# Bias seeded into PSUM by ScalarE, and the last batches reordered, in a two-layer graph attention kernel

## The chip, the cores and the metric

The kernel runs on one core of a Trainium2 chip. The metric is the device time in microseconds of one execution; lower is better. The engines are named as in the profile: PE (TensorE, matrix products), DVE (VectorE), ACT (ScalarE), POOL (GpSimd), SP (SyncE, which here issues nearly all DMAs). Each engine works through its own instructions in program order [...].

## The reference, cut to what matters

The input `x` holds 128 batches of 128 tokens with 512 features, all in 32-bit floats. With `B = 128`, `L = B - 1` and `ln` a normalization over the features without weights, the reference computes for every batch:

```
y  = ln(x + relu(max_over_features(adj @ x) + b))       # layer 0
q, k, v = split(y @ w_qkv)                              # 8 heads of 64
p  = softmax(where(adj == 0, -inf, q k^T / 8))
o  = concat_heads(p v) @ w_proj + b_proj
z  = y + o + ln(o) * gamma + beta                       # layer 1
out = ln(z)
```

Only the last part of this concerns the change: the projection `o`, its bias `b_proj`, the inner normalization of `o`, the residual sum, and the outer normalization of `z`.

## The kernel before, in words

Batches go in groups of four (`G = 4`, `NG = 32` groups). The products with the weights are done for a whole group by a scheme that replaces eight block products by seven (class `Unit`, lines 165 to 194): `product(i)` adds one of seven products into one of the PSUM banks `b1` to `b4`, `snap(k)` copies the running sum in `b1` to SBUF on ACT, and `result(half, col)` adds a bank and a snap on DVE. The left operands of a unit for `o` are sums of blocks that POOL makes (`o_sums`, line 495).

For one batch `scores` (line 385) makes the scores on PE, `softmax_max` adds the mask and takes the maximum on DVE, `softmax_exp` runs one exponential per head on ACT, `softmax_div` divides on DVE, `prob_transpose` transposes 32 by 32 blocks on DVE, `prob_write` and `prob_read` finish the transposition through DRAM with DMAs on SP's queue, `attend` (line 471) multiplies with `v` on PE and `attend_copy` copies the result to SBUF on ACT. `prob_move` is the three middle steps together; its read waits on SP for its write to land, and everything later on SP waits with it.

The end of a batch is a row of tail steps. `bn` and `finish_stats` (lines 245 to 269) take mean and variance on DVE and turn them into a scale and a shift, mostly on POOL, where `ALU.pow` gives the inverse root. `tail_inner_one` (line 599) normalizes `o` on ACT, `tail_residual_one` (line 603) has three steps on POOL: times gamma, plus `o`, plus the saved row that a DMA has brought back. `tail_outer_one` (line 622) normalizes `z` on ACT and stores it. For the very last batches `fused_open` and `fused_close` (lines 608 to 620) do the inner normalization and the residual sum on DVE instead.

A loop over pairs of batches (line 730) does this until four pairs from the end, with the bias added by POOL. The last part, from line 888, is written out by hand: a list of calls whose order is the order of the instructions on each engine, since `pin` keeps program order. There the bias is added on PE: `biased` (line 891) follows products 2, 5 and 4 of the units `o_u` with two products each of a row of ones and the bias, and `last_project` (line 518), which projects one of the last four batches alone, ends with `add_bias` (line 515). Before those, `last_load` (line 509) and ten `tail_reload_one` calls bring `w_proj` and ten saved rows into one buffer, through SP's queue.

PSUM has eight tiles by tag: `b1` to `b4` of the units, `pss0`, `pss1`, `po`, `pa` of scores and attention. A new tile of a tag waits until the old one has been read. The last four batches are projected into `b2`, `pss0`, `pss1` and `b1`.

The order of the tails before the change: the statistics `last_1` (line 962) take two rows of `z` and four of `o` together, ahead of `attend(L - 5)`; then normalizing and residual steps of L-11 to L-8 in the next stretch, L-5 and L-4 after `attend(L - 2)`, L-7 and the fused L-3, L-2, L-6, L-1 and L to the end.

Of the kernel before, what the change touches and what calls it, by code (L numbers as in the profile page):

```python
# [16 lines left out]
def kernel(  # L17
# [55 lines left out]
    def pe(*args, **kwargs):  # L73
        pin(nc.tensor.matmul(*args, **kwargs))  # L74

    def tt(eng, dst, a, b, op):
        pin(eng.tensor_tensor(dst, a, b, op))  # L77
# [71 lines left out]
    make_identity(nc, ident)  # L149
    mhalf = const.tile([P, 1], F32, name="mhalf")  # L150
    pin(nc.gpsimd.memset(mhalf, -0.5))
    ones = const.tile([1, P], F32, name="ones")
    pin(nc.gpsimd.memset(ones, 1.0))

# [8 lines left out]
    class Unit:  # L165
# [6 lines left out]
            self.banks, self.snaps = {}, {}  # L172

        def product(self, i):
            bank, first = {1: (1, True), 6: (1, False), 7: (1, False), 2: (2, True),
                           5: (3, True), 3: (3, False), 4: (4, True)}[i]
            if first:
                self.banks[bank] = psum.tile(
                    [P, 2, HT], F32, tag=f"b{bank}", name=f"b{bank}_{self.name}"
                )  # L180
            self.mm(self.banks[bank], i - 1, self.lefts[i], first)

        def snap(self, k):
            t = sb.tile([P, 2, HT], F32, tag=f"u{k}", name=f"u{k}_{self.name}")
# [200 lines left out]
    def scores(b, banks=("pss0", "pss1")):  # L385
        g, h, jj = place(b)
        pss[b] = [
            psum.tile([P, NP, P], F32, tag=tag, name=f"pss{par}_{b}")
            for par, tag in enumerate(banks)
        ]  # L390
        for pr in range(NP):
            for par in range(2):
                t = qk[g, pr // 2, h][ds(par * HD, HD), :, pr % 2, ts(jj, P)]
                pe(pss[b][par][:, pr], lhsT=t[:, 0], rhs=t[:, 1], start=True, stop=True)
# [71 lines left out]
    def prob_move(b):  # L466
        prob_transpose(b)
        prob_write(b)
        prob_read(b)
# [15 lines left out]
    def attend_copy(b):  # L485
        g, h, jj = place(b)
        if jj == 0:
            tag = "x" if (g, h) == (NG - 2, 0) else "oT"
            oT[g, h] = sb.tile([P, KC, HT], F32, tag=tag, name=f"oT_{g}_{h}", bufs=2)
        pin(nc.scalar.copy(oT[g, h][:, :, ts(jj, P)], pos.pop(b)))  # L490
# [15 lines left out]

    def last_load():
        t = sb.tile(WQK, F32, tag="wqk", name="wlast")  # L510
        w = t[:, :2].rearrange("p a b e -> p (a b) e")
        pin(nc.sync.dma_start(out=w, in_=w_proj.rearrange("(c p) e -> p c e", p=P)))
        return w, t[:, 2:].rearrange("p a b e -> p (a b) e")

    def add_bias(dst, cols):
        pe(dst, lhsT=ones, rhs=bp_bc[0:1, cols], start=False, stop=True, skip_group_check=True)

    def last_project(b, w, tag):
        g, h, jj = place(b)
        ps = psum.tile([P, D], F32, tag=tag, name=f"pp_{b}")  # L520
        for c in range(KC):
            pe(
                ps,
                lhsT=oT[g, h][:, c, ts(jj, P)],
                rhs=w[:, c],
                start=c == 0,
                stop=True,
                skip_group_check=True,
            )
        add_bias(ps, slice(0, D))  # L530
        os_[b] = ps


    zs, xr = {}, {}
# [92 lines left out]
    def stats(name, *items, eng=None, fused=0):  # L627

        mv = small.tile([P, NC, 2], F32, tag="mv", name=f"mv_{name}")
        for k, (kind, b) in enumerate(items):  # L630
            bn({"o": o_of, "z": zs.get, "y": xs.get}[kind](b), mv, k)
        finish_stats(mv, items, eng, fused)
        return mv


    for f, tag in enumerate(("pa", "po", "b3", "b4")):
# [250 lines left out]

    L = B - 1
    po_pa = ("po", "pa")

    def biased(unit, i):

        unit.product(i)
        bank, cols = {2: (2, slice(0, HE)), 5: (3, slice(HE, D)), 4: (4, slice(0, HE))}[i]
        for k in range(2):
            add_bias(unit.banks[bank][:, k], cols)


    before, o_u, v_u = second, o_unit(NG - 3), v_unit(NG - 1)
# [2 lines left out]
    attend_copy(L - 7)  # L902
    attend(L - 6, "pa")
    attend_copy(L - 6)
    scores(L - 5)
    scores(L - 4, po_pa)
    before.result(1, 1)
# [3 lines left out]
    softmax_max(L - 4)  # L911
    o_u.product(1)
    o_u.snap(1)
    biased(o_u, 2)
    softmax_exp(L - 5)
    o_u.result(0, 0)
    before.product(3)
    before.result(0, 1)
    tail_residual(B // 2 - 7)
    o_u.product(6)  # L920
    scores(L - 3)
    softmax_exp(L - 4, range(4))
    o_u.snap(2)
    softmax_exp(L - 4, range(4, H))
    softmax_div(L - 5)
    prob_move(L - 5)
    biased(o_u, 5)
    softmax_max(L - 3)
    scores(L - 2, po_pa)
    biased(o_u, 4)  # L930
    o_u.product(7)
    softmax_exp(L - 3, range(4))
    o_u.snap(3)
    softmax_exp(L - 3, range(4, H))
# [9 lines left out]
    for t in range(L - 9, L + 1):  # L944
        tail_reload_one(t, room[:, t - L + 9])
    v_u.product(2)
    v_u.product(1)
    v_u.snap(1)
    o_u.product(3)
    softmax_exp(L - 2, range(4))  # L950
    o_u.result(0, 1)
    v_u.result(0, 0)
    v_u.product(6)
    v_u.snap(2)
    softmax_exp(L - 2, range(4, H))
    v_u.product(5)
    v_u.product(4)
    v_u.product(7)
    softmax_div(L - 3)
    prob_transpose(L - 3)  # L960
    prob_write(L - 3)
    stats(
        "last_1",
        ("z", L - 13), ("z", L - 12), ("o", L - 11), ("o", L - 10), ("o", L - 9), ("o", L - 8),
    )


    attend(L - 5)
    v_u.snap(3)
    attend_copy(L - 5)  # L970
    attend(L - 4, "pa")
    attend_copy(L - 4)
    prob_read(L - 3)
    scores(L - 1)
    v_u.result(1, 1)
    run_sums(o_sums(NG - 2))
    for t in range(L - 11, L - 7):
        tail_inner_one(t)
    softmax_max(L - 1)
    scores(L, po_pa)  # L980
    v_u.result(1, 0)
    o_u = o_unit(NG - 2)
    o_u.product(1)
    o_u.snap(1)
    biased(o_u, 2)
    softmax_div(L - 2)
    prob_move(L - 2)
    softmax_exp(L - 1)
    softmax_max(L)
    o_u.result(0, 0)  # L990
    v_u.product(3)
    v_u.result(0, 1)
    for t in range(L - 11, L - 7):
        tail_residual_one(t)
    o_u.product(6)
    softmax_exp(L, range(4))
    o_u.snap(2)
    softmax_exp(L, range(4, H))
    biased(o_u, 5)
    biased(o_u, 4)  # L1000
    o_u.product(7)
    softmax_div(L - 1)
    prob_move(L - 1)
    softmax_div(L)
    prob_move(L)
    attend(L - 3)
    o_u.snap(3)
    attend_copy(L - 3)
    attend(L - 2, "pa")
    attend_copy(L - 2)  # L1010
    tail_outer(B // 2 - 7)
    tail_store(B // 2 - 7)
    mv = small.tile([P, NC, 2], F32, tag="mv", name="mv_last_2")
    keys = [("z", L - 11), ("z", L - 10), ("o", L - 5), ("o", L - 4)]
    bn(zs[L - 11], mv, 0)
    bn(zs[L - 10], mv, 1)
    o_u.result(1, 1)
    o_u.result(1, 0)
    bn(o_of(L - 5), mv, 2)
    bn(o_of(L - 4), mv, 3)  # L1020
    pool = nc.gpsimd
    finish_stats(mv, keys, pool)
    for t in (L - 5, L - 4):
        tail_inner_one(t)
    for t in (L - 11, L - 10):
        tail_outer_one(t)
    tail_residual_one(L - 5, [0])
    o_u.product(3)
    o_u.result(0, 1)
    last_project(L - 3, wlast, "b2")  # L1030
    last_project(L - 2, wlast, "pss0")
    attend(L - 1)
    attend(L, "pa")
    mv2 = stats("last_3", ("o", L - 6), ("o", L - 7), eng=pool, fused=1)
    tail_inner_one(L - 7)
    tail_residual_one(L - 5, [1])
    mv = stats("last_4", ("o", L - 3), ("z", L - 9), eng=pool, fused=1)
    tail_outer_one(L - 9)
    fused_open(L - 3, mv[:, 0, 0:1])
    tail_residual_one(L - 5, [2])  # L1040
    fused_close(L - 3)
    attend_copy(L - 1)
    attend_copy(L)
    last_project(L - 1, wlast, "pss1")
    last_project(L, wlast, "b1")
    tail_residual_one(L - 4, [0])
    mv = stats("last_5", ("o", L - 2), ("z", L - 3), ("z", L - 8), eng=pool, fused=1)
    fused_open(L - 2, mv[:, 0, 0:1])
    for t in (L - 3, L - 8):
        tail_outer_one(t)  # L1050
    tail_residual_one(L - 4, [1, 2])
    fused_open(L - 6, mv2[:, 0, 0:1])
    fused_close(L - 2)
    fused_close(L - 6)
    tail_residual_one(L - 7, [0])
    mv = stats("last_6", ("o", L - 1), ("z", L - 2), ("z", L - 5), eng=pool, fused=1)
    fused_open(L - 1, mv[:, 0, 0:1])
    for t in (L - 2, L - 5):
        tail_outer_one(t)
    tail_residual_one(L - 7, [1, 2])  # L1060
    fused_close(L - 1)
    mv = small.tile([P, NC, 2], F32, tag="mv", name="mv_last_7")
    keys = [("o", L), ("z", L - 1), ("z", L - 4), ("z", L - 6)]
    for k in (2, 3, 1):
        bn(zs[keys[k][1]], mv, k)
    bn(o_of(L), mv, 0)
    finish_stats(mv, keys, pool, fused=1)
    fused_open(L, mv[:, 0, 0:1])
    for t in (L - 1, L - 4, L - 6):
        tail_outer_one(t)  # L1070
    fused_close(L)
    stats("last_8", ("z", L), ("z", L - 7), eng=pool)
    for t in (L, L - 7):
        tail_outer_one(t)


# [39 lines left out]
```

## Time and profile before

| | |
|---|---|
| median of 3 runs | 1969.37 us (1969.04 to 1970.28) |
| profiled execution, its own time | 1968.16 us |
| span of the profiled execution | 1966.4 us |
| granted TensorE clock, mean | 0.997 |
| busy share of the span: PE, DVE, ACT, POOL | 99%, 80%, 54%, 66% |
| last product on PE starts | 1950.69 us |
| last instruction on ACT starts | 1962.09 us |

The times of the profile are microseconds from the start of the span. A row of a timeline has the start, the duration, the engine, the line of the code (often that of a helper: line 74 is every product, line 77 every tensor-tensor operation), the operation, the tile written and the tiles read, the shape, how many instructions are merged into the row, and in brackets how long the engine was idle before it and what released it. Products of 32-bit operands appear as two instructions each. In rows of groups, "busy us, mean ns" is the total and the duration of one.

### The profile page before, as it was taken

The numbers are of one execution on the slowest core, as the hardware profiler recorded it, in microseconds if no ns is written. First come the engines' busy times: TensorE is split into PE (matmuls) and PEld (weight loads), VectorE is DVE, ScalarE is ACT, GpSimd is POOL, SyncE is SP. The second block draws the span as 40 slices with busy tenths as digits, with TensorE's granted clock in tenths as the row PEclk, the third lists the DMA queues.
The fourth block names the chain that finished last, engine by engine and source line by source line (L and its number), as shares of the span: only waits on it lengthen the run. The fifth ranks groups of instructions, "written<-read, shape, count | busy, mean of one in ns | idle before, by whom it ended". The sixth has DMA issues, their size and how long they took to land.

```text
span 1966.4 us, 33091 instructions
## 1 busy us (share of the span) xinstructions
PE 1945.3 (99%) x11575; PEld 1642.5 (84%) x11575; DVE 1564.2 (80%) x2516; ACT 1054.6 (54%) x3066; POOL 1294.2 (66%) x815
## 2 busy tenths in 40 slices
PE   9999999999999999999999999999999999999996
PEld 6888888888888888888888888888888888888883
DVE  6767878878778778788788787787787887877777
ACT  3444654655555546546556555555465465555463
POOL 6336766767666767667676667676676776676737
PEclk9999999999999999999999999999999999999998
DMA  7647567576576676676675765765766766757544
GB/s 223 169 121 191 145 177 193 155 189 175 164 197 162 168 200 160 169 194 157 185 189 157 191 167 166 203 161 164 198 157 180 189 161 187 174 162 189 150 167 144
DMA packets 445654, 341.75 MB, mean 174 GB/s; under 512 B 276912, under 2 KB 378416, under 8 KB 445488
## 3 DMA queue, kind: packets, MB, share of 16 engines
q1 hardware_dynamic: 445056, 338.85, 64.4%
q8 instruction: 92, 1.51, 0.3%
q10 hardware_dynamic: 432, 0.79, 0.1%
q14 instruction: 74, 0.61, 0.1%
HBM read 172.82 MB, written 166.72 MB: 173 GB/s over the span
## 4 chain that ended last, share of the span: by engine, by line
PE 95%; DVE 2%; POOL 2%; DMA 0%; ACT 0%; issue 0%; SPq 0%; ACTq 0%; POOLq 0%; DVEq 0%
PE b_qk L74 40%; PE b_v L74 19%; PE b_o L74 19%; PE pss L74 6%; PE po L74 6%; PE pa L74 5%; POOL zl L77 1%; DVE st_mv_last L247 1%; POOL s_o L77 0%; POOL rs_mv_last L77 0%; DMA x<-in_x_dram 0%; PE idle L74 0%; DVE mv_last L248 0%; ACT s L419 0%; DVE z L620 0%
## 5 line engine op out<-in xcount | busy, mean ns | idle before, releaser
L74 PE MATMUL b_qk<-s_x,wqk 128*128 128x256 f32 x2048 | 473.4, 379 | 0.6 <-DVE s_x L77 0.3
L74 PEld LDWEIGHTS b_qk<-s_x,wqk 128*128 128x128 f32 x2048 | 388.8, 190 | 55.1 <-issue 0.9
L419 ACT ACTIVATE s<-s,nmax 128x128 f32<-128x128 f32 x1024 | 396.1, 391 | 6.7 <-DVE nmax L412 6.7
L74 PE MATMUL b_qk<-x1T,wqk 128*128 128x256 f32 x1536 | 358.8, 383 | 0.1
L74 PEld LDWEIGHTS b_qk<-x1T,wqk 128*128 128x128 f32 x1536 | 286.6, 190 | 45.2 <-issue 1.0
L77 POOL TENSOR_TENSOR z<-z,ga_bc 128x1024 f32<-128x1024 f32 x58 | 164.5, 2836 | 168.5 <-ACT z L273 168.5
L259 POOL TENSOR_SCALAR rs_mv<-mv 128x6 f32<-128x6 f32 (+2 forms) x61 | 14.7, 241 | 380.9 <-DVE mv L248 380.9
L77 DVE TENSOR_TENSOR s<-s,rec 128x1024 f32<-128x1024 f32 x128 | 252.9, 1976 | 4.4
L185 ACT COPY u_qk<-b_qk 128x512 f32<-128x512 f32 x192 | 112.4, 585 | 245.4 <-PE b_qk L74 244.1
L74 PE MATMUL b_v<-wv,s_x 128*128 128x256 f32 x1024 | 237.0, 379 | 0.0
L74 PE MATMUL b_o<-wp,s_o 128*128 128x256 f32 x992 | 230.1, 380 | 0.5 <-DVE v L191 0.5
L74 PEld LDWEIGHTS b_v<-wv,s_x 128*128 128x128 f32 x1024 | 194.4, 190 | 26.8 <-issue 0.3
L191 DVE TENSOR_TENSOR qk<-b_qk,u_qk 128x512 f32<-128x512 f32 x256 | 168.2, 675 | 56.7 <-PE b_qk L74 44.4
L400 DVE SCALAR_TENSOR_TENSOR s<-pss,mask 128x512 f32<-128x512 f32 x256 | 164.3, 684 | 59.4 <-PE pss L74 59.1
L74 PEld LDWEIGHTS b_o<-wp,s_o 128*128 128x128 f32 x992 | 188.1, 190 | 27.2 <-DVE v L191 0.9
L77 POOL TENSOR_TENSOR x<-x,be_bc 128x1024 f32<-128x1024 f32 x64 | 181.3, 2834 | 33.5 <-DVE rec L430 27.4
L419 ACT ACTIVATION_READ_ACCUMULATOR s<-s,nmax 128x1 f32 x1024 | 193.9, 189 | 0.0
L191 DVE TENSOR_TENSOR v<-b_v,u_v 128x512 f32<-128x512 f32 x128 | 87.1, 681 | 133.9 <-PE po L74 129.1
L185 ACT COPY u_o<-b_o 128x512 f32<-128x512 f32 x93 | 54.4, 585 | 247.0 <-PE b_o L74 247.0
L185 ACT COPY u_v<-b_v 128x512 f32<-128x512 f32 x96 | 56.2, 585 | 238.4 <-PE b_v L74 238.4
L74 PE MATMUL b_v<-wv,x1T 128*128 128x256 f32 x768 | 176.2, 379 | 0.0
L74 PEld LDWEIGHTS b_v<-wv,x1T 128*128 128x128 f32 x768 | 145.9, 190 | 32.2 <-issue 13.9
(115 smaller groups left out, 3403.9 us busy)
## 6 DMA issues: line engine op xcount, KB each, us to landing
hop<-pu SPq DMA_DIRECT2D x128, 512.0 KB, 3.4
pT<-hop SPq DMA_DIRECT2D x512, 128.0 KB, 3.7
spill<-x SPq DMA_DIRECT2D x64, 512.0 KB, 4.8
x<-in_x_dram SPq DMA_DIRECT2D x62, 512.0 KB, 4.4
xhop<-xt SPq DMA_DIRECT2D x248, 128.0 KB, 2.3
x1T<-xhop SPq DMA_DIRECT2D x248, 128.0 KB, 3.9
xr<-spill SPq DMA_DIRECT2D x59, 512.0 KB, 3.5
out_dram<-xr SPq DMA_DIRECT2D x58, 512.0 KB, 4.1
```

Of the source, the lines that this page charges most:

```text
L74: pin(nc.tensor.matmul(*args, **kwargs))
L77: pin(eng.tensor_tensor(dst, a, b, op))
L185: pin(nc.scalar.copy(t, self.banks[1]))
L191: nc.vector.tensor_tensor(self.out[half, col], self.banks[bank], self.snaps[k], ALU.add)
L247: pin(nc.vector.bn_stats(st, src))
L259: pin(nc.gpsimd.tensor_scalar(rs[:, :n], mv[:, :n, 1], EPS, None, ALU.add))
L400: nc.vector.scalar_tensor_tensor(s[:, par], pss[b][par], SCALE, mask.unsqueeze(1).to_broadcast([P, NP, P]), ALU.mult, ALU.add,)
L419: nc.scalar.activation(prob[b][:, i], prob[b][:, i], AF.Exp, bias=nmax[b][:, i : i + 1], accum_out=psums[b][:, i : i + 1],)
```

## The change

The row of ones goes. ScalarE writes the bias into a PSUM bank before the products, [...] no product into such a bank carries the start flag. `seed` does so for banks 2, 4 and 3 of the two last `o_u` units, `last_seed` for the banks of the last four batches, which are now `b2`, `b4`, `b3` and `b1`.

Two statistics of `z` (L-8 and L-11) are taken on ACT: `scalar_stats` runs an Identity with a sum, a mean, and a Square of the deviation with a sum, and `finish_scalar_stats` ends them on POOL. The outer normalization of the last batch goes from ACT to DVE (`tail_outer_vector`). The hand-written list is reordered. The inner normalization and the residual steps of L-9 and part of those of L-8 move ahead of `attend(L - 5)`; the statistics are cut into more and smaller groups that POOL finishes; `softmax_div(L - 2)` and its transposition and write come before `attend(L - 5)`; the scores of L-2 and of L come earlier; `attend(L - 1)` and `attend(L)` come ahead of `last_project(L - 2)`, and their copies come behind the statistics on ACT. L-8 and L-11, then L-10, are normalized later than before.

```diff
-    def add_bias(dst, cols):
-        pe(dst, lhsT=ones, rhs=bp_bc[0:1, cols], start=False, stop=True, skip_group_check=True)
-
-    def last_project(b, w, tag):
+    def seed(unit, bank):
+        cols = slice(HE, D) if bank == 3 else slice(0, HE)
+        bias = bp_bc[:, cols].unsqueeze(1).to_broadcast([P, 2, HE])
+        pin(nc.scalar.copy(unit.new_bank(bank), bias))
+
+    def last_seed(b, tag):
+        os_[b] = psum.tile([P, D], F32, tag=tag, name=f"pp_{b}")
+        pin(nc.scalar.copy(os_[b], bp_bc))
...
-                start=c == 0,
+                start=False,
...
-        add_bias(ps, slice(0, D))
-        os_[b] = ps
...
+    def tail_outer_vector(b, mean):
+        z, (rs, _) = zs.pop(b), stat_of.pop(("z", b))
+        pin(nc.vector.tensor_scalar(z, z, mean, rs, ALU.subtract, ALU.mult))
+        pin(nc.sync.dma_start(out=out[b], in_=z))
+
+    def scalar_stats(*batches):
...
+        for k, b in enumerate(batches):
+            pin(act(trash, zs[b], AF.Identity, accum_out=sums[:, k : k + 1]))
+        pin(act(mean[:, :n], sums[:, :n], AF.Identity, scale=-1.0 / D))
+        for k, b in enumerate(batches):
+            pin(
+                act(
+                    trash, zs[b], AF.Square, bias=mean[:, k : k + 1], accum_out=dev[:, k : k + 1]
+                )
+            )
+        return batches, mean, dev
+
+    def finish_scalar_stats(stat):
+        batches, sh, rs = stat
+        n = len(batches)
+        pin(nc.gpsimd.tensor_scalar(rs[:, :n], rs[:, :n], 1.0 / D, EPS, ALU.mult, ALU.add))
+        tt(nc.gpsimd, rs[:, :n], rs[:, :n], mhalf.to_broadcast([P, n]), ALU.pow)
+        tt(nc.gpsimd, sh[:, :n], sh[:, :n], rs[:, :n], ALU.mult)
...
+    seed(o_u, 2)
     scores(L - 5)
...
-    biased(o_u, 2)
+    o_u.product(2)
     softmax_exp(L - 5)
+    seed(o_u, 4)
...
+    softmax_exp(L - 4, range(4))
     o_u.product(6)
     scores(L - 3)
-    softmax_exp(L - 4, range(4))
+    scores(L - 2, po_pa)
     o_u.snap(2)
+    seed(o_u, 3)
     softmax_exp(L - 4, range(4, H))
     softmax_div(L - 5)
     prob_move(L - 5)
-    biased(o_u, 5)
+    o_u.product(4)
+    o_u.product(5)
+    o_u.product(7)
     softmax_max(L - 3)
-    scores(L - 2, po_pa)
-    biased(o_u, 4)
-    o_u.product(7)
...
+    stats("last_1", ("o", L - 9), ("o", L - 8), eng=pool)
...
+    for t in (L - 9, L - 8):
+        tail_inner_one(t)
+    tail_residual_one(L - 9)
     v_u.product(5)
-    v_u.product(4)
     v_u.product(7)
+    stats("last_2", ("o", L - 11), ("o", L - 10), eng=pool)
+    tail_residual_one(L - 8, [0])
     softmax_div(L - 3)
...
+    softmax_div(L - 2)
+    prob_transpose(L - 2)
+    prob_write(L - 2)
...
+    o_u.product(5)
+    o_u.product(7)
     softmax_exp(L, range(4, H))
-    biased(o_u, 5)
-    biased(o_u, 4)
-    o_u.product(7)
+    o_u.snap(3)
+    o_u.product(4)
...
+    o_u.product(3)
+    o_u.result(0, 1)
+    last_project(L - 3, wlast)
+    for t, tag in ((L - 2, "b4"), (L - 1, "b3"), (L, "b1")):
+        last_seed(t, tag)
+    attend(L - 1)
+    attend(L, "pa")
+    last_project(L - 2, wlast)
+    stat = scalar_stats(L - 8, L - 11)
+    finish_scalar_stats(stat)
     for t in (L - 5, L - 4):
         tail_inner_one(t)
...
     attend_copy(L - 1)
     attend_copy(L)
-    last_project(L - 1, wlast, "pss1")
-    last_project(L, wlast, "b1")
+    last_project(L - 1, wlast)
+    last_project(L, wlast)
...
     mv = small.tile([P, NC, 2], F32, tag="mv", name="mv_last_8")
     keys = [("o", L), ("z", L - 1), ("z", L - 4)]
...
+    mv = small.tile([P, NC, 2], F32, tag="mv", name="mv_last_9")
+    bn(zs[L], mv, 0)
+    finish_stats(mv, [("z", L)], pool, fused=1)
+    mv2 = small.tile([P, NC, 2], F32, tag="mv", name="mv_last_10")
+    bn(zs[L - 7], mv2, 0)
+    finish_stats(mv2, [("z", L - 7)], pool)
+    tail_outer_vector(L, mv[:, 0, 0:1])
+    tail_outer_one(L - 7)
```

## The prediction

> **What bounds the kernel now.** I read the busy table by stage first, then the order of instructions on each engine from 1869 us on, where the change begins. Columns of the table: stretch, its length, busy us of PE, weight loads, DVE, ACT, POOL, granted clock, DMA share, GB/s.
>
> ```profile
> 1870.00:1904.00 34.00, 34.00 (x220) 28.12 (x216) 25.37 (x36) 19.87 (x76) 7.07 (x3) 1.00 0.39 133
> 1904.00:1952.00 48.00, 44.71 (x245) 27.69 (x244) 40.55 (x69) 22.12 (x56) 42.39 (x46) 1.00 0.54 183
> 1952.00:1966.40 14.40, 0.00 (x0) 0.00 (x0) 7.20 (x16) 5.26 (x7) 6.57 (x11) 0.58 0.34 128
> ```
>
> The reader sees three stages. To 1904 PE never rests and POOL is idle four fifths of the time. To 1952 PE rests 3.3 us, and POOL (42.4 of 48) and DVE (40.6) are nearly as full. After 1952 PE has nothing left: 14.4 us of statistics, normalizing and stores. The PE timeline has these rows (start, duration, what):
>
> ```profile
> 1884.99 1.12 PE L74 MATMUL b_o<-bp_bc,ones 1*128 1x256 f32 x4
> 1886.05 1.16 PE L74 MATMUL pss<-qk 64*128 64x128 f32 x16
> ...
> 1942.38 3.70 PE L74 MATMUL pp<-wlast,oT 128*128 128x512 f32 x8 [2.62 <-ACT oT L490]
> ...
> 1950.69 1.12 PE L74 MATMUL pp<-bp_bc,ones 1*128 1x512 f32 x2
> ```
>
> From start to start a group of bias products takes 1.06 us, and the last one ends PE's work at 1951.8. POOL's timeline:
>
> ```profile
> 1878.69 2.37 POOL L77 TENSOR_TENSOR xr<-xr,z 128x1024 f32<-128x1024 f32 x1
> 1906.12 0.25 POOL L259 TENSOR_SCALAR rs_mv_last<-mv_last 128x6 f32<-128x6 f32 x1 [25.07 <-DVE mv_last L248]
> ...
> 1916.76 1.27 POOL L77 TENSOR_TENSOR zl<-zl,xr 128x512 f32<-128x512 f32 x1
> 1917.98 2.25 POOL L77 TENSOR_TENSOR zl<-zl,ga_bc 128x512 f32<-128x512 f32 x1
> ```
>
> POOL waits 25 us for the statistics "last_1", then works almost without a gap to 1955. So past 1906 two queues end close together: PE, and POOL with DVE. SP's queue is a serial chain too:
>
> ```profile
> 1899.44 7.20 SPq L555 DMA_DIRECT2D wlast<-spill  x10
> 1907.05 0.32 SPq L449 DMA_DIRECT2D hop<-pu  x1
> 1914.91 1.74 SPq L460 DMA_DIRECT2D pT<-hop  x4
> ...
> 1928.06 0.34 SPq L449 DMA_DIRECT2D hop<-pu  x1
> 1931.51 1.73 SPq L460 DMA_DIRECT2D pT<-hop  x4
> ```
>
> Each read waits on SP until its write has landed: 7.9 us behind the loads, 3.5 later.
>
> [...] At 512 elements with two pointers [...] the trace has 801 to 809, and 1283 for its one load. [...] the 2.25 us row above, against 1.27, ran beside a softmax division (s times rec) that took 2.10 instead of 1.23.
>
> **The change part by part.**
>
> Bias products. Removed from PE: six groups b_o x 1.06 = 6.4 and four groups pp x 1.06 = 4.2, together 10.6 us, all on PE's path. Added on ACT: six seeds and four last seeds. No row has SBUF to PSUM; the nearest is the copy PSUM to SBUF, 0.585, [...] the slow end is the 0.80 of normalizing. I take 0.6 (ends 0.5 and 0.8): 6 us. ACT is busy 22 of 48 us, so this costs nothing by itself; uncovered it is 6 us. The waits matter: a seed waits for the result that frees its bank, with snaps and exponentials queued behind it. By the walk the seeds of bank 2 and 4 find theirs free; bank 3's second seed waits on v_u.result(0,1) (DVE, 1909.9) while ACT reaches it at 1911.9.
>
> First part, to 1904. Three bias groups gone: v_u.product(2) starts at 1888.8 instead of 1891.95. The earlier scores(L-2) waits for nothing (DVE freed its banks at 1878.3). The third snap moves from 1892.15 to 1888.7, so exponentials (4 x 0.385) and the two normalizings (1.42) end at 1892.1, not 1895.6. SP then stands at the read of L-4, to 1893.2; its store and all loads go 2.45 us earlier: the first one-batch reload is issued at 1897.0 and, at 6.3 to land, is there at 1903.3.
>
> POOL. Statistics of L-9 and L-8 come straight after their results (DVE 1894.0), normalizing at 1897.6, and the first two residual steps of L-9 run in the idle time. Its third step adds the reloaded row and waits to 1903.3. From there POOL is continuous: third steps and others of L-9, L-8, L-11, L-10, L-5, L-4, L-7, 19 x 1.31 (start to start of free rows) = 24.9; contention with the last two softmax divisions 2 x 0.95 = 1.9; o_sums 4 x 1.3 = 5.2; finishing last_2 1.65, last_3 1.85, last_4 1.65, the ScalarE statistics 1.4, last_5 2.0, last_6 2.05, last_7 2.2 = 12.8 (power rows: 0.72, 0.87, 1.03 for 2, 3, 4 columns, 0.3 for each small operation). Sum 44.8: L-7's residual ends at 1948.1. In the kernel before the same step ends at 1955.0.
>
> ACT and VectorE, 1903 to 1925. ACT stands at normalizing L-11 and L-10 until POOL has finished last_2 (1904.6 + 1.65 = 1906.3); four exponentials, the first snap, bank 4's seed and four more exponentials are queued behind it, and end at 1911.9. That wait is new, and PE feels it: product(6) waits for the snap and for o_sums' second row (0.5), product(5) for bank 3's seed (0.5). VectorE goes two score passes (2.46 each, from 1903.8), three results, last_3's three statistics (0.79 each), division and transposition of L-1 to 1916.3 and of L to 1921.0 (2.8 free, 3.5 beside POOL), then the results that free banks 4 and 3 at 1921.6 and 1923.8. The last seeds of L-2, L-1 and L wait for those and end at 1925.1; behind them on ACT stand the ScalarE statistics, and PE needs the first of them only after attend(L).
>
> ScalarE statistics. [...] ending about 1928.4 when POOL wants them at 1928.6. Square has no row: nothing if its table is loaded, 1.3 if not; I take 0. They take two statistics, 1.6 us, off DVE; the last normalizing, of L, goes from ACT (0.81) to DVE (nearest row 0.75). The two attend copies stand behind them, and behind normalizing L-5 and L-4 (to 1930.4).
>
> SP and the last attention. Two writes go out together at 1904.6, two reads follow from 1912.5 to 1916.0. L-1: write 1917, read 1920.6 to 1922.3. L: write 1922.4, read 1925.9 to 1927.7, landed 1930.6 (3.0 to land). PE comes to attend(L) at 1926.5: a new wait of 4 us, since last_project(L-2) now stands behind it. Then 1.0 + 3.7 + 3.6 + 3.6: PE ends at 1942.5, 9.3 earlier. Moved stores and reloads keep their number on SP.
>
> End. VectorE can't take o of L before fused_close(L-1), which needs POOL's last_7: it gets there at 1945.9, so PE has 3.4 us of slack and POOL decides. After 1948.1: last_8's power 1.3, fused_close 0.75, statistics 0.9, last_9 with one column 1.0, last_10 1.5, ACT 0.8: 1954.3. Before, the last ACT instruction ended at 1962.9 and the span at 1966.4: 3.5 for store and end, so 1957.8; one contended fused_close (1.75 seen against 0.75) for 0.6: **1958.4**. That is 8.0 under the span of 1966.4. The profiled execution took 1968.16, 1.76 around its span; it becomes 1960.2. The median of the runs, 1969.37, is 1.2 above it: 1969.4 - 8.0 = **1961.4 us**.
>
> **Rivals.**
> PE decides. If POOL has no further say, PE's end at 1942.5 plus the 11.7 us that the kernel before needed from o(L)'s statistics (1954.72) gives 1954.2: 12.2 saved, 1957.2 us. For: POOL spans are rough. Against: the sum on POOL above.
> Contention eats it. Eleven VectorE instructions of the tail have two SBUF inputs (four divisions, five fused_close, two of L-6); I counted two or three. Six more at 0.95 on POOL leave 2.3: 1967.1 us. Against: before, only some of them collided.
> Slower: the reload holds POOL. L-9's third step now stands ahead of o_sums, so a late reload delays product(6), all exponentials and the end, one for one. It decides past 1903.3 + 8.0 + 3.9 = 1915.2. If the 4.3 MB from the store on had to land together, at the 196 GB/s of the trace's 1910 to 1930 stretch, that is 22 us from 1896: 1918, 14.7 late, 1976 us. Against: reloads landed 5.5 to 7.0 after issue.
> That the seeding doesn't do what it says would alter values and leave the queues as they are; it moves no time.
>
> **How the numbers follow.** The POOL walk 0.55 (its own range 1957.4 to 1965.4); PE decides 0.20; contention 0.17, of which 0.05 still saves over 0.2%; reload 0.08. 0.2%, 3.9 us, is about what a measurement of this kernel can tell from no change. Faster 0.80, same 0.12, slower 0.08. The range 1956.0 to 1967.2 takes in both neighbours' values and leaves out the reload case and the edges.
>
> **What would show it.** Right: no row of bp_bc,ones; seeds near 0.6; POOL's wait before 1906 mostly gone and its L-9 third step released by a DMA near 1903; an attend(L) released by DMA near 1930; PE's end near 1942; VectorE or POOL, not PE, releasing the last steps. Wrong: a reload after 1908, POOL rows of 2.2 throughout, a second table load, or ACT idle on seeds for over 2 us.

## The result, and the profile after

The median of four runs is 1967.66 us (1965.58 to 1968.01), against 1969.2 us (1968.37 to 1970.28) in four runs of the kernel before: ratio 0.999, 95% interval 0.9972 to 1.0007. In 21 further runs of the same program (after_again below) the median is 1966.94 against 1969.47: ratio 0.9987, interval 0.998 to 0.9993. So the change saves some 2 us, 0.1%. In the longer row of runs the interval leaves out 1, so the saving is real, but it is under the 0.2% that the prediction took as the least that can be told from no change. Forecast were 1961.4 us, with a range from 1956.0 to 1967.2.

Two lengths have to be kept apart. The **last part** runs from the first product of attend(L-7), with which the change begins, to the end of the span. Before, it started at 1869.73 and took 1966.4 - 1869.73 = 96.67 us; in a second trace of the kernel before (before_again) 96.94. After, it started at 1872.27 and took 1965.7 - 1872.27 = 93.43; in after_again 93.86. That is 3 us less, and it repeats. The **first part**, which both kernels share, doesn't: in thirteen traces of all kernels here it took from 1869.7 to 1873.3 us. The profiled execution of the kernel before had the shortest of all, that of the changed kernel 2.54 us more. All times after are therefore compared by their distance from the start of the last part.

The busy table of the changed kernel, by the stages shown for the kernel before, moved by those 2.54 us (stretch, length, busy us of PE, weight loads, DVE, ACT, POOL, clock, DMA share, GB/s):

```profile
1872.54:1906.54 34.00, 32.97 (x252) 28.61 (x249) 26.64 (x38) 24.30 (x85) 11.00 (x9) 1.00 0.38 123
1906.54:1954.54 48.00, 35.55 (x186) 23.49 (x182) 39.80 (x71) 27.70 (x71) 42.09 (x49) 0.93 0.57 193
1954.54:1965.70 11.16, 0.00 (x0) 0.00 (x0) 3.87 (x8) 2.33 (x3) 5.58 (x12) 0.50 0.37 140
```

Over the first two stages PE's work fell from 78.7 to 68.5 us, close to the 10.6 us that the ten bias groups took; 9.2 of it is in the middle stage. POOL's did not fall there: 42.1 of 48 us, and now it is the fullest engine, ahead of VectorE with 39.8. POOL's timeline (start, duration, what, and in brackets the idle time before and its releaser):

```profile
1897.45 0.23 POOL L261 TENSOR_SCALAR rs_mv_last<-mv_last 128x2 f32<-128x2 f32 x1 [13.32 <-DVE mv_last L250]
...
1901.81 1.27 POOL L77 TENSOR_TENSOR zl<-zl,ga_bc 128x512 f32<-128x512 f32 x1 [2.75 <-ACT zl L275]
1903.16 1.26 POOL L77 TENSOR_TENSOR zl<-zl,o 128x512 f32<-128x512 f32 x1
1908.76 1.27 POOL L77 TENSOR_TENSOR zl<-zl,wlast 128x512 f32<-128x512 f32 x1 [4.33 <-DMA wlast<-spill]
```

The long wait for last_1 is shorter, the first two residual steps of L-9 run early, and then POOL stands 4.3 us for the reloaded row. After that row POOL waits only once before the statistics of L, 0.69 us for the ScalarE statistics. What made the row late is in the chain that ended last (start, duration, what):

```profile
1894.87 0.30 SPq L462
...
1896.71 4.66 DMA out_dram<-xr
1901.38 0.34 SPq L557
...
1902.25 6.38 DMA wlast<-spill
...
1908.76 1.27 POOL zl L77
...
1914.26 1.28 POOL s_o L77
...
1915.59 7.21 PE b_o L74 x24
```

The chain goes through the store of the pair 56, whose buffer the reload of the pair 58 takes over, through the reload of L-9, and through POOL into the sums that product(6) needs. On PE the new waits are these:

```profile
1915.59 7.19 PE L74 MATMUL b_o<-wp,s_o 128*128 128x256 f32 x24 [2.29 <-POOL s_o L77]
...
1935.70 1.09 PE L74 MATMUL po<-pT,v 128*64 128x128 f32 x16 [2.91 <-DMA pT<-hop]
1936.72 10.57 PE L74 MATMUL pp<-wlast,oT 128*128 128x512 f32 x24
```

Behind the first of these waits the granted clock was 0.50 from 1917 to 1920, and the 24 rows took 7.19 us; in e5_both and e8_fill_both (below), which have no wait there, they took 5.43 and 5.44. PE is done at 1947.3, 75.0 into the last part, where it was 82.1 before (77.3 in after_again). VectorE takes the statistics of o(L) at 1953.21, 5.9 us later. PE's saving of 7 us meets a queue that isn't there yet.

### The profile page after: what moved, and what is told of

It is laid out like the page before. It is cut to its first block, busy times and chain, and to the rows that moved or that the text cites. A ratio compares the mean times of both kernels' runs of the same rounds, so it can differ in the third digit from the quotient of the medians.

```text
span 1965.7 us, 33048 instructions
## 1 busy us (share of the span) xinstructions
PE 1936.3 (99%) x11543; PEld 1639.7 (83%) x11543; DVE 1560.8 (79%) x2512; ACT 1062.2 (54%) x3084; POOL 1296.1 (66%) x824
## 4 chain that ended last, share of the span: by engine, by line
PE 95%; DVE 2%; POOL 1%; DMA 1%; ACT 0%; issue 0%; SPq 0%; POOLq 0%; ACTq 0%; DVEq 0%
PE b_qk L74 39%; PE b_v L74 19%; PE b_o L74 18%; PE pss L74 6%; PE po L74 6%; PE pa L74 6%; POOL zl L77 1%; DMA x<-in_x_dram 0%; DMA wlast<-spill 0%; DVE s L77 0%; POOL rs_mv_last L77 0%; PE idle L74 0%; DVE pu L442 0%; DMA out_dram<-xr 0%; DVE s L402 0%
## 5 line engine op out<-in xcount | busy, mean ns | idle before, releaser
L193 DVE TENSOR_TENSOR qk<-b_qk,u_qk 128x512 f32<-128x512 f32 x256 | 168.0, 675 | 57.1 <-PE b_qk L74 44.8
```

Source lines behind the costliest of these rows:

```text
L193: nc.vector.tensor_tensor(self.out[half, col], self.banks[bank], self.snaps[k], ALU.add)
```

## The experiments

The theory after reading the trace: POOL's queue, started by the reload of L-9, ends last, and PE's gain is hidden behind it. The rivals: PE decides, or VectorE's wait for the buffer of v (3.29 us, found in the trace), or PE's wait at attend(L). All lengths of the last part come from one trace each, and two traces of one program differ by 0.3 to 0.4 us; the ratio is to runs of the kernel before that were timed with each.

| kernel | median us | ratio, 95% interval | last part |
|---|---|---|---|
| before, before_again | 1969.71, 1969.49 | 1.0001, 0.9992 to 1.001 | 96.67, 96.94 |
| changed, after_again | 1967.66, 1966.94 | 0.9987, 0.998 to 0.9993 (after_again) | 93.43, 93.86 |
| e1_seeds_only | 1968.29 | 0.9991, 0.9983 to 0.9999 | 94.36 |
| e2_order_only | 1970.12 | 0.9999, 0.9991 to 1.0008 | 97.23 |
| e3_loads_first | 1965.55 | 0.9979, 0.997 to 0.9987 | 91.41 |
| e4_result_late | 1967.47 | 0.9988, 0.9981 to 0.9995 | 92.66 |
| e5_both | 1964.91 | 0.9977, 0.9971 to 0.9984 | 91.47 |
| e6_ones_kept | 1967.53 | 0.9992, 0.9984 to 1.0001 | 93.45 |
| e7_pool_less | 1964.26 | 0.9973, 0.9963 to 0.9983 | 90.96 |
| e8_fill_both | 1963.85 | 0.9969, 0.9958 to 0.9981 | 90.05 |
| e9_fill_alone | 1966.08 | 0.998, 0.9973 to 0.9986 | 92.76 |

**The two halves of the change alone.** First the seeds in the old order:

```diff
+    seed(o_u, 2)
     scores(L - 5)
...
-    biased(o_u, 2)
+    o_u.product(2)
...
     attend_copy(L - 2)
+    for t, tag in ((L - 3, "b2"), (L - 2, "pss0"), (L - 1, "pss1"), (L, "b1")):
+        last_seed(t, tag)
...
-    last_project(L - 3, wlast, "b2")
+    last_project(L - 3, wlast)
```

> The order of before, with the ten bias groups on PE replaced by ten ScalarE copies into PSUM. Theory A (past 1906 us POOL's queue decides, and it starts when the statistics last_1 are done): PE is 3.2 us ahead there, so POOL starts 3.2 us sooner and the end comes about 3 us sooner than in the kernel before; PE's own end moves by about 10 us and leaves a wait between it and the end. Theory B (PE decides): about 10 us less than before.

Measured: 94.36, which is 2.3 to 2.6 less than before, and far from B's 10; theory A. The statistics last_1 reach POOL at 1906.84 - 1873.04 = 33.8 into the last part, against 36.4 before, 2.6 earlier, and the end follows by about as much. PE's end came 4.9 us earlier, at 77.2, and not the 10 that the expectation names: in the old order PE stands twice for a seed on ScalarE (1.57 and 1.39 us). The chain that ended last in this kernel runs on POOL almost without a break from here on:

```profile
1907.17 1.36 POOL rs_mv_last L77
...
1908.80 1.23 POOL s_o L77
1910.11 4.73 POOL s_o L77 x3
...
1914.84 1.23 POOL zl L77
```

Then the new order with the bias on PE:

```diff
-    seed(o_u, 2)
...
-    o_u.product(2)
+    biased(o_u, 2)
...
-    last_seed(L - 3, "b2")
...
-                start=False,
+                start=c == 0,
...
+        add_bias(os_[b], slice(0, D))
```

> The order of the changed kernel, with the bias still added by products on PE. Theory A (the chain store, reload, POOL, sums for the o unit decides, and PE has waits that take up most of the bias products): 2 to 3 us slower than the changed kernel, so about level with the kernel before. Theory B (PE decides): about 10 us slower than the changed kernel.

Measured: 97.23, 3.4 to 3.8 over the changed kernel and 0.3 to 0.6 over the kernel before. The number is nearer to A than to B, a little more than A said, but A's reason isn't what this trace shows. The chain that ended last runs on PE up to 1922 and not through the reload, for which POOL waits only 1.6 us here. Later it comes back to PE at attend(L):

```profile
1936.01 1.98 PE L74 MATMUL po<-pT,v 128*64 128x128 f32 x16 [1.88 <-DMA pT<-hop]
1937.92 5.67 PE L74 MATMUL pp<-wlast,oT 128*128 128x512 f32 x8
```

The clock was 0.50 from 1936 to 1941 here, and the eight rows took 5.67 us instead of 3.70; VectorE waits 4.3 us for them. PE's end is at 83.3. So with the bias on PE in the new order PE decides, and the seeds are worth 3.4 to 3.8 us there, 2.3 to 2.6 in the old order. The reordering alone costs 0.3 to 0.6, hardly more than two traces differ, and adds 0.5 to 0.9 to the seeds.

**The reload.** The loads go ahead of the store, and the reload that needs the stored buffer goes behind the writes of probabilities:

```diff
     tail_outer(B // 2 - 8)
-    tail_store(B // 2 - 8)
-    tail_reload(B // 2 - 6)
     wlast, room = last_load()
     for t in range(L - 9, L + 1):
         tail_reload_one(t, room[:, t - L + 9])
+    tail_store(B // 2 - 8)
...
     prob_write(L - 2)
+    tail_reload(B // 2 - 6)
```

> The changed kernel with the ten one-batch reloads and the weight load issued ahead of the store of the pair 55, and the reload of the pair 58, which reuses the stored buffer, behind the two writes of probabilities. Theory A (the reload of L-9, queued behind that store's landing of 4.7 us, holds POOL): POOL's third step of L-9 starts 4 us sooner or when its own queue lets it, and the end comes about 3 us sooner than in the changed kernel. Theory B (VectorE's wait of 3.3 us ahead of the division of L-2, or ScalarE's waits, take over): under 1 us.

The expectation calls the stored pair 55; it is the pair 56. Measured: 91.41, 2.0 to 2.4 less than the changed kernel. POOL's timeline has no wait for the row any more:

```profile
1903.31 1.27 POOL L77 TENSOR_TENSOR zl<-zl,o 128x512 f32<-128x512 f32 x1
1904.65 1.28 POOL L77 TENSOR_TENSOR zl<-zl,wlast 128x512 f32<-128x512 f32 x1
```

The third step starts 32.3 into the last part, against 36.5: the 4 us are there, the end took half of them. Theory A holds for the cause and overstates the gain: POOL now waits 1.21 us for VectorE at one place, and PE stands 3.69 us ahead of attend(L), so another chain takes over (below).

**VectorE's wait for the buffer of v.** The tile of v has two buffers, and the half that v_u.result(1, 1) fills is the one that attend(L - 4) still reads. The changed kernel puts that result ahead of the division of L-2, and VectorE stands:

```profile
1906.06 0.69 DVE L193 TENSOR_TENSOR v<-b_v,u_v 128x512 f32<-128x512 f32 x1 [3.29 <-PE po L74]
```

The edit moves it behind the write of L-2:

```diff
     v_u.product(4)
-    v_u.result(1, 1)
     softmax_div(L - 2)
     prob_transpose(L - 2)
     prob_write(L - 2)
+    v_u.result(1, 1)
```

> The changed kernel with the result that fills the second half of the last v moved behind the division, transposition and write of L-2, so that VectorE doesn't stand 3.3 us waiting for attend(L-4) to free the buffer of v. Theory A (VectorE's chain is not the one that ends last while POOL waits for the reload): within 1 us of the changed kernel. Theory B (that wait is the loss): about 3 us less.

Measured: 92.66, 0.8 to 1.2 less than the changed kernel; at the edge of A's bound, and not B's 3. With both edits:

> The changed kernel with both edits, loads ahead of the store and the last v's result behind the division of L-2. Theory A (two waits in parallel chains hold the changed kernel, the reload on POOL and the v buffer on VectorE, and each hides the other): the last part is 89 to 90 us, 3.5 to 4.5 less than in the changed kernel and more than the 2.0 and 0.8 of the two edits alone together. Theory B (POOL's sum of work decides once the reload is early): no better than the loads alone, 91.4.

Measured: 91.47, the number of theory B and not of A: the second edit adds nothing to the first. But B's reason is not seen either. In this trace POOL waits 1.7 us for VectorE, VectorE 3.2 us for PE, and PE stands 3.98 us ahead of attend(L). What follows on PE is slow:

```profile
1933.45 1.98 PE L74 MATMUL po<-pT,v 128*64 128x128 f32 x16 [3.98 <-ACT oT L492]
1935.36 12.42 PE L74 MATMUL pp<-wlast,oT 128*128 128x512 f32 x24
```

```profile
1930.00:1935.00 5.00, 1.55 (x15) 1.58 (x16) 2.56 (x5) 3.40 (x7) 3.74 (x9) 0.73 0.80 257
1935.00:1940.00 5.00, 5.00 (x12) 2.13 (x9) 2.66 (x6) 2.71 (x4) 4.76 (x5) 0.59 0.30 108
```

The eighth column of this second table is the granted clock: 0.73 and 0.59 in the ten microseconds after PE ran dry. The last three projections took 12.42 us, where e3 has 11.18 and the changed kernel's first trace 10.57. So the loss of clock, 1.2 us more than in e3, may hide what the second edit brings; its worth with early loads isn't shown. The wait ahead of this stretch was 3.98 us, but the clock also fell to 0.50 behind the wait of 1.88 us in e2 and that of 2.29 us in the changed kernel.

**POOL's load, directly.** Three multiplications by gamma are left out (part of the computation is missing, so the time is that of a lighter POOL only):

```diff
-    tail_residual_one(L - 5)
+    tail_residual_one(L - 5, [1, 2])
...
-    tail_residual_one(L - 4)
+    tail_residual_one(L - 4, [1, 2])
...
-    tail_residual_one(L - 7)
+    tail_residual_one(L - 7, [1, 2])
```

> The changed kernel without the multiplication by gamma in the residual steps of L-5, L-4 and L-7: three POOL steps of 1.31 us less, which leaves out part of the computation. Theory A (POOL's queue decides to the end): the last part is 3 to 3.9 us shorter than in the changed kernel, near 90. Theory B (the chain of PE, transposition and attention decides): under 0.7 us.

Measured: 90.96, 2.5 to 2.9 less for 3.9 us of POOL work, far from B's 0.7 and short of A's 3. What holds the rest was not tested by a run of its own: in this trace PE waits 3.0 us for the DMA at attend(L), with a mean clock of 0.66 from 1935 to 1940, after it, and POOL then waits 1.5 and 0.7 us for VectorE, so the chain through attend(L) probably takes over at about 91, as in e3 and e5.

**Filling PE's wait.** The projection of L-2 goes between the two attentions, on top of e5 and alone:

```diff
     attend(L - 1)
+    last_project(L - 2, wlast)
     attend(L, "pa")
-    last_project(L - 2, wlast)
```

> The kernel with both edits (loads first, the last v's result late) and the projection of L-2 moved ahead of attend(L), where PE stood idle for 4 us waiting for the transposed probabilities of L, after which its granted clock was down to 0.59 for 5 us and the last three projections took 12.4 us instead of 10.6. Theory A (that wait and the lower clock after it decide once the reload is early): the last part falls from 91.5 to 88 or 89 us, with a clock of 0.9 or more throughout. Theory B (POOL's sum decides there too): 91 or more.

Measured: 90.05, 1.4 less than e5, with a clock of 1.00 up to 1940:

```profile
1928.62 3.70 PE L74 MATMUL pp<-wlast,oT 128*128 128x512 f32 x8
1932.38 1.09 PE L74 MATMUL po<-pT,v 128*64 128x128 f32 x16
1933.41 7.13 PE L74 MATMUL pp<-wlast,oT 128*128 128x512 f32 x16
```

PE ends 68.2 into the last part, 6.8 earlier than in e5. The direction is A's, the gain is less than its 88 to 89; at 90.05 POOL holds the end again: from its first residual step at 1901.92 to 1955.75 its only wait is one of 0.69 us. This is the fastest complete kernel of the study: 1963.85 us, ratio 0.9969.

> The changed kernel with only the projection of L-2 moved ahead of attend(L). Theory A (in the changed kernel POOL, held by the reload, ends last, and PE's wait at attend(L) is hidden): within 0.6 us of its last part of 93.4 to 93.9. Theory B (PE's wait decides there): 2 us or more less.

Measured: 92.76, 0.7 to 1.1 less, a little over A's bound and far from B's 2. PE's end moved by 3.7 to 6.0 us, so most of that was hidden.

**What repeats, and the first part.**

> The changed kernel once more, for its last part and its start in more executions. The last part, from attend(L-7)'s first product to the end of the span, took 93.4 us against 96.7 in the kernel before: if that is the change, it is 93.4 within 0.7 again; if the trace of the changed kernel caught a chance, it isn't. The median stays 1.5 to 3 us under the kernel before.

Measured: 93.86, as expected, with a median 2.5 us under the kernel before. The row of L-9 came later in this trace: POOL's third step started 37.1 us into the last part.

> The kernel before once more, for a second trace of its last part, which took 96.7 us in the first: 96.7 within 0.5 if this part repeats, whatever the first part of the span does.

Measured: 96.94, as expected.

> The changed kernel with the unused row of ones and its memset on POOL left in. Theory A (the medians of the first part differ by chance or by where the runs fell): same median as the changed kernel within 0.7 us. Theory B (without the memset something at the start moves, so that the first part takes 1.3 us longer): 1.3 us under the changed kernel, with a last part of 93.4 us in both cases.

Measured: a median of 1967.53 against 1966.94, theory A: no sign that leaving out the memset costs 1.3 us. The last part is a third trace of the changed kernel's: 93.45. In it the store freed its buffer in 4.22 us and POOL's third step of L-9 started at 35.7 instead of 36.5, yet the end came no earlier. POOL later waited 1.09 us for VectorE, VectorE 2.55 us for PE, and PE had stood 4.22 us at attend(L), with a clock of 0.50 behind it and 12.17 us for the 24 rows that took 10.57 in the first trace. So in this trace PE's wait came last and not the reload, by about a microsecond. The two chains end close together in the changed kernel: filling the wait alone gains 0.7 to 1.1 us (e9), the early loads alone 2.0 to 2.4 (e3), and all three edits together 3.4 to 3.8 (e8).

The first rows of PE show where the first part differs; before, then after:

```profile
7.24 2.84 PE L74 MATMUL pa<-x,adjT 128*128 128x512 f32 x6 [1.13 <-DMA x<-in_x_dram]
```

```profile
8.16 4.54 PE L74 MATMUL pa<-x,adjT 128*128 128x512 f32 x6 [1.99 <-DMA x<-in_x_dram]
```

The load of x came 0.9 us later, and the same six instructions took 1.7 us more. In other traces they took 2.84 to 5.49 us, in kernels with the memset and without. The load itself came at 7.24 and 7.37 in the two traces of the kernel before and at 8.05 to 8.47 in all eleven others, with the memset too (e2, e6). Why is not shown; it may be part of the reason that the medians saved less than the last part did.

## Why the prediction was wrong, by its own steps

The method was right in its choice of queue and wrong in two terms of the sum, the time of the reload and the length of POOL's work. Counted from the start of the last part, the forecast end was 1958.4 - 1869.73 = 88.7 and the measured one 93.4. The 4.7 us between split up as follows.

- **Bias products and seeds: right.** No row of bp_bc,ones is left, the six seeds took 0.584 each and the four last seeds 0.586, where 0.6 was taken. ScalarE stood 2.2 us ahead of the last seeds for results on VectorE, just over the 2 us that the prediction had named as a sign of being wrong. The change counts on the products adding to what ScalarE wrote. The reference sets `b_proj` to zeros, so no run here shows that they do; the runs show the times alone.
- **The reload: wrong by 2.9.** The forecast let POOL's third step of L-9 start at 33.6; it started at 36.5. The step that failed is "its store and all loads go 2.45 us earlier": it let the store free its buffer as fast as in the kernel before. SP's rows there (start, duration, what) show 2.83 us from the store to the reload that waits for it:

```profile
1891.93 1.73 SPq L460 DMA_DIRECT2D pT<-hop  x4
1895.75 0.40 SPq L579 DMA_DIRECT2D out_dram<-xr  x1
1898.58 0.34 SPq L549 DMA_DIRECT2D xr<-spill  x1
```

In the changed kernel the store went out earlier (24.4 into the last part, against 26.0 before), but behind the four reads of L-4, which ended 0.9 us later than forecast, and it took 4.66 us: it now stands directly behind those reads on SP, where 2.1 us lay between them before. So 0.9 of the 2.9 is the store's start, 1.8 its landing and 0.2 the rest.

In before_again the store took 2.82; in five more traces with the order of the changed kernel (after_again, e4, e6, e7, e9) 4.13 to 5.13. It isn't the order that does it: in e1, with the old order, there is no pause behind the reads either, and the store took 4.52; in e2, with the new order, there are 1.9 us of pause, and it took 3.05. The trace of the kernel before could have told: the store ahead of this one, 0.1 us behind eight reads, took 4.33 (1863.94 to 1868.27), and the median of its 58 stores of this size is 4.1 from issue to landing.

So the reloads were issued at 30.0, and at 29.7 in the kernel before: the advance was gone. The landing time of the reload itself, 6.38, was as forecast. This is the rival "the reload holds POOL", given 0.08: right in its place, and far smaller than the 14.7 us it was priced at. (Its 4.3 MB are a slip: from the store on there are 4.7, 512 + 512 + 1024 + 10 x 256 KB.)

- **POOL's sum: wrong by 2.5.** Forecast 44.8 from that step to the end of L-7's residual; measured 1908.76 to 1956.05, 47.3. Of this 0.9 are the residual rows: three were contended and not two, 2.14 and 2.14 us beside softmax divisions of 1.72 and 1.30 on VectorE and 1.83 beside a fused_close of 0.72, against 1.27 for the free ones, which is 0.4, and the free ones follow each other at 1.34 and not 1.31, which is 0.5. The finishing steps are 1.1: the shift on line 268 took 0.79 to 0.80 three times within this sum, where 0.3 was taken for each small operation (the kernel before has such rows too, 0.79 and 0.80), and the power of the ScalarE statistics took 1.05 instead of 0.72. The wait for ScalarE is 0.7: its statistics ended 62.1 into the last part, where the forecast of 58.7 was the author's estimate (an Identity took 0.59 to 0.60 us, a Square 0.69 and the reading of each sum 0.19). The o_sums were 0.2 shorter. No single row stands out: without the wait, fifty rows took 4% more than forecast.
- **The end: 0.7 better**, 9.65 against 10.3. 2.9 + 2.5 - 0.7 = 4.7.
- **A wait that was missed.** VectorE's 3.29 us for the buffer of v: the working took the result for one that only needs its bank and its snap. It cost about 1 us here (e4), since the reload hid the rest; with the loads early no gain showed (e5), in a trace where PE's clock fell further.
- **PE's slack: right in kind.** Forecast 3.4 us between PE's end and VectorE's need of it, measured 5.9, with PE's end at 75.0 instead of 72.8. Attend(L) was released by a DMA, as said: 63.4 instead of 60.9, after a wait of 2.9 instead of 4. Ahead of product(6) PE waited 2.29 where 0.5 was forecast, and behind that its clock was 0.50 from 1917 to 1920. A lower clock after a wait was not in the forecast.
- **PE decides**, given 0.20, is refuted for the changed kernel by e9, and for the old order by e1: PE's end moved by 3.7 to 6.0 and by 4.9 us, the kernel's end by 0.7 to 1.1 and by 2.3 to 2.6. **Contention eats it**, given 0.17, came in a small part: one contended residual row more than counted, not six. Whether the three long shifts are contention too was not tested; each started 0.05 us after a fused_close did (1937.52, 1944.42 and 1950.92). In the kernel before, the five POOL rows of 128x512 past 1906 that took 1.59 to 2.26 us ran beside a softmax division (three) or a fused_close (two), which are among those that the prediction counts by their two SBUF inputs.

Of the 8 us that were forecast, then, some 3 came in the last part, and 1.5 to 2.5 in the medians. The first part varies by 3.6 us from trace to trace, more than the whole saving.

What stays open: how the reads hold the store. By the rates of the traces 0.52 MB moved between the store's issue and its buffer coming free in the two traces of the kernel before, which is the store itself, and 0.90 MB in the first trace of the changed kernel (0.89 in e1). The 0.37 MB beyond the store fit the reads ahead of it, 4 x 128 KB, an estimate from these rates alone. Whether the store queues behind them or shares the DMA engines with them was not measured apart.

## What to carry to other kernels

Work taken from the engine at 99% gives only as much as the next queue leaves: sum that queue row by row, and doubt a sum of many small rows, which came out 4% short here. Take the time of a DMA from a place where it stands as it will stand after the change, and not from the one before it moves (the store took 2.83 us before and 4.66 after). A step that is moved into idle time brings its inputs' deadlines with it; here the input was a DMA whose issue hung on a store's landing, on a queue in which the change had just closed the pause ahead of it. Before moving a result earlier, look at who still reads the buffer that it overwrites, and if a wait on PE can't be avoided, put other products into it, because the clock fell to 0.50 after seven of the eight waits at attend(L) listed below: the projection of L-2 in the wait for L brought PE's end 3.7 to 6.8 us forward (e9, e8).

## What the runs showed of the hardware that was not expected

These waits of PE were followed by a granted clock of 0.50 for some microseconds: at attend(L) after 3.23 us in after_again, 3.69 in e3, 3.95 in e4, 3.98 in e5, 4.22 in e6, 2.98 in e7 and 1.88 in e2, and at product(6) after 2.29 us in the first trace of the changed kernel. After 2.91 us at attend(L) in that same trace, and after 2.62 and 2.65 in the two traces of the kernel before, the clock stayed at 1.00. So here the length of one wait didn't tell whether the clock would fall. The lowest mean clock over 5 us behind the waits at attend(L) was 0.74 in after_again, 0.76 in e3, 0.67 in e4, 0.59 in e5 and 0.66 in e7. The 24 product rows that followed took 10.57 us at 1.00, in the first trace of the changed kernel, and 11.27, 11.18, 12.26, 12.42 and 12.26 in these five, 12.17 in e6; in e2 the first eight took 5.67 us and the next eight 3.70.

A store of 512 KB freed its buffer 2.8 to 3.1 us after its issue with 2 us of pause ahead of it (three traces), and 4.1 to 5.1 us directly behind four reads of 128 KB (seven traces). Square on ScalarE needed no table load after the exponentials: the trace of the changed kernel has one load, of 1.28 us, at 2.13.
